# A graph layer with sorted edges: the first nodes' words loaded earlier and in two parts, a group of nodes multiplied tile by tile, the last group scaled from PSUM

## The chip, the cores and the metric

The kernel runs on one core of a Trainium2 chip. A core has five queues of instructions that work side by side: TensorE (PE, matrix products into PSUM), VectorE (DVE), ScalarE (ACT), GpSimd (POOL) and SyncE (SP, which here issues DMAs). The metric is the device time of one execution in microseconds, as the median of several.

## What is computed

The input is a graph of 12,500 nodes with 128 numbers each and 412,500 directed edges (200,000 random pairs in both directions, and a loop at every node). The edges are sorted by their target node `dst`. Cut to what matters, with all constant factors left out:

```
f0 = x[:, :32] @ W1_0e            f1 = x[:, 32:] (as 32 x 3) @ W1_1o
feat0, self0 = halves of f0       feat1, self1 = halves of f1
e0, e1 = feat0[src], feat1[src]                          # a gather, one row an edge
h = gelu(gelu(edge_attr_8 @ W_mlp1) @ W_mlp2)            # edge weights
w00, w01, w10, w11 = h @ Wp_00, h @ Wp_01, h @ Wp_10, h @ Wp_11
mid0 = [w00 * e0 * a0,   w11 * sum(e1 * a1)]             # a0, a1: edge_attr_4
mid1 = [w01 * e0 * a1,   w10 * e1 * a0]
n0, n1 = segment_sum(mid0, dst), segment_sum(mid1, dst)  # sums by target node
y = [cos * self0 + sin * (n0 @ W2_0e),  cos * self1 + sin * (n1 @ W2_1o)]
out = layernorm(x + y)
```

## The kernel before

**Pieces.** The sorted edges are cut into 806 runs of 512 (`SB`) edges; the last run has 340. Four runs (`CH`) make a chunk, so there are 202 chunks (`NCH`), and the nodes are cut into 25 groups of 512 (`GN`), each of four tiles of 128; the last group has 128 + 84 nodes. A loop over steps `s` (L946) takes one run a step; `c, k = divmod(s, CH)`.

**Setup** (L897 to L941) is a loop over `b` from 0 to 26. Step `b` turns the nodes of group `b` with TensorE, multiplies those of group `b - 1` by the feature weights, stores those of group `b - 2` to the `table` in DRAM through ScalarE's queue, and loads the nodes of group `b + 6` through SP. From `b = 5` on it also takes one load from the list that `weight_loads` makes (L908, L924), and at some steps one extra piece of work: `load_raws(0)` at 4, `load_indices(0)` at 12, `make_w1b` at 15, `tile_places` at 21 (L910 to L914). Meanwhile GpSimd gathers the rows of the first 18 runs straight from `x`. After setup it gathers from `table`, up to 18 runs ahead of the run in work; the order of the instructions on PE, ACT, DVE and SP is the order of the program (L896).

**A step of the main loop.** GpSimd gathers the rows of run `s + 18`, four gathers of 128 rows; in some runs a column of 128 rows comes instead from ScalarE or VectorE, which copy single columns out of the transposed nodes `xT` (L190, L192), or from single-row DMAs on SP (L209). TensorE makes the edge weights of later runs (L521 to L569). VectorE multiplies weights and gathered rows into messages `M` (L637, L641), and TensorE sums the messages of run `s - 1` by target node (L666, L668). Where in the sums the 128 edges of a column begin is read from `tile_first`, the first target node of each column; the relative node of an edge, `rel`, lies in 0 to 7 (`J` = 8) and picks one of eight places. Per chunk, VectorE adds the sums of 96 nodes to an accumulator of 768 nodes (L681) at `first_at`, the first node of the chunk less a base.

**Groups of nodes.** When the last edges of a group are in, `norm` multiplies its nodes: `moments` (L687) makes one TensorE product with `xT` (L698) and four with the accumulator (L701) for each tile, into one PSUM tile, and ScalarE copies that to SBUF (L706, L708). Later `statistics` takes mean and variance (L714, L715), `deviations` the root, and `normalise` scales the tiles on ScalarE (L742; for the last group, every second on VectorE, L739) and stores them through SP (L744). Group 23, the last but one, is multiplied at chunk 200, and group 24 after the last chunk, in `norm_last`.

**One buffer used several times in setup.** `scratch` (L319) is the first buffer of the accumulator, 128 rows of 4 x 768 words. Until the main loop's step 1 it holds what setup needs:

```
return scratch[:, part, :SB]                                        # L446 rows_tile(part)
raws[b] = [load_run_rows(dst, b, NO_NODE, None if b else 0), ...]   # L449 load_raws: dst in part 0, src in part 1
return scratch.rearrange("p a n -> p (a n)").bitcast(dtype)[0:1, i * NCH:(i + 1) * NCH]   # L323 line(i)
first_node = line(0, I32)                                           # L325
```

`load_raws(0)` brings the targets of runs 0 to 127, one run a row. `load_indices(0)` casts them to floats (L457), subtracts the first of each 128 (L460) and turns them into `rel`. `first_node` holds the first target of each of the 202 chunks and is read by `find_first` at step 1 (L402).

**The branch at the end.** The scheme needs edges sorted by target, with at most eight different nodes in 128 edges. `load_indices` counts the edges that break this: words below the first of their 128 (L461) and words at least 7.5 above it (L463), both into `odd`; `find_first` and `tile_places` count places out of range. `count_odd` sums the counts (L783), and at the end

```
with tc.If(n_odd > padded):    # L1041
    general()
```

where `padded` is 44, the words that fill up the last run. `general` (L788) does all edges again in any order: it zeroes sums in DRAM, runs a loop over 412,500 / 125 = 3,300 passes (L805), each of which loads 125 edges (L810 to L813), gathers their rows (L822) and the old sums (L880), makes weights and messages, and scatters the new sums (L884), and then normalises all groups again.

Of the kernel before, what the change touches and what calls it, by code (L numbers as in the profile page):

```python
# [25 lines left out]
Q = 4  # L26
# [25 lines left out]
COL_Q = {DVE: Q - 2, ACT: Q - 3}  # L52
COL_FROM = {DVE: 12, ACT: 12}
LNB = 2
TURN_AT = (7, 9, 11, 13, 15, 17, 18, 20, 22, 24)


@with_exitstack
def gnn_kernel(ctx: ExitStack, tc: tile.TileContext, x, src, dst, ea4, ea8, w1_0, w1_1, wm1, wm2,
# [26 lines left out]
    def sub(ap, offset, dims):  # L86
        return bass.AP(tensor=ap.tensor, offset=ap.offset + offset, ap=dims)
# [248 lines left out]

    def weight_loads():

        yield w1r, sub(wm1, 0, [[0, P // RAD], [HID, RAD], [1, HID]])
        yield w2b, sub(wm2, 0, [[0, 2], [HID, HID], [1, HID]])  # L340
        for j, w in enumerate((wp00, wp01, wp10, wp11)):
            yield wpb[:, j * MUL:(j + 1) * MUL], sub(w, 0, [[0, 2], [MUL, HID], [1, MUL]])
        for t, w in ((w20, w2_0), (w21, w2_1)):
            yield t[:MUL, :], w[:MUL, :]
            yield t[MUL:, :], sub(w, MUL * MUL, [[0, 3], [MUL, MUL], [1, MUL]])
        yield first_node, sub(dst, 0, [[1, 1], [CH * SB, NCH]])
        for b, t in enumerate(tile_first):
            c0, n = b * P, t.shape[0]
            last = c0 + n == NCH and E < NCH * CH * SB
            if last:  # L350
                yield (t[n - 1:n, :].rearrange("a (k o) -> a k o", o=1),
                       sub(dst, (NCH - 1) * CH * SB, [[1, 1], [0, CH * Q], [1, 1]]))
                k = -(-(E - (NCH - 1) * CH * SB) // P)
                yield t[n - 1:n, :k], sub(dst, (NCH - 1) * CH * SB, [[k * P, 1], [P, k]])
            yield t[:n - last], sub(dst, c0 * CH * SB, [[CH * SB, n - last], [P, CH * Q]])

    def make_w1b():

# [31 lines left out]
    assert all(len(bs) == 1 for c, bs in due.items() if c < NCH - 1)  # L390
    assert N - base[-1] + SPAN <= ACC and ACC - GN <= GN
    first_at = cst.tile([1, NCH], I32)
    NT = -(-NCH // P)
    tile_first = [cst.tile([min(P, NCH - b * P), CH * Q], I32, name=f"tf{b}") for b in range(NT)]

    def find_first():

        floor, strays = line(1), line(2)
        steps = [(0, 0)] + [(c + 1, (bs[-1] + 1) * GN) for c, bs in due.items() if c + 1 < NCH]
        for (r, n0), (z, _) in zip(steps, steps[1:] + [(NCH, 0)]):  # L400
            nc.vector.memset(floor[:, r:z], float(n0))
        nc.vector.tensor_tensor(floor, first_node, floor, op=OP.subtract)  # L402
        nc.vector.tensor_scalar(strays, floor, 0.0, float(ACC - SPAN), op0=OP.max, op1=OP.min)
        nc.vector.tensor_copy(first_at, strays)
        nc.vector.tensor_tensor(strays, strays, floor, op=OP.not_equal)
        nc.vector.tensor_reduce(odd[0:1, 2 * NB:2 * NB + 1], strays, axis=mybir.AxisListType.X, op=OP.add)

    def tile_places():

        for b, t in enumerate(tile_first):  # L410
# [233 lines left out]

    def places(c):

        b, r = divmod(c, P)
# [34 lines left out]


    pend, done = [], []
    before_last = due[NCH - 1][0] - 1

    def moments(b, sums=None):  # L687
        n0, nn, full, tail, tiles = group(b)
        if not pend:
            Y["y"] = wk.tile([P, LNB, XB, P], F32, name="y", bufs=1)  # L690
            Y["v"] = wk.tile([P, LNB * XB, 2], F32, name="mv")
            nc.vector.memset(Y["v"], 1.0)
        j = len(pend)
        pend.append(b)
        pt = ps.tile([P, XB, P], F32, name="h")
        at = n0 - base[-1] if b in due[NCH - 1] else 0
        for t, k in tiles:
            nc.tensor.matmul(pt[:k, t, :], xT[:, n0 + t * P:n0 + t * P + k], ws, start=True, stop=sums is not None)  # L698
            if sums is None:
                for a in range(4):  # L700
                    nc.tensor.matmul(pt[:k, t, :], A["now"][:, a, at + t * P:at + t * P + k], wpost[:, a, :],  # L701
                                     start=False, stop=a == 3)
            else:
                nc.vector.tensor_tensor(pt[:k, t, :], pt[:k, t, :], sums[:k, t, :], op=OP.add)
        if full:
            nc.scalar.activation(Y["y"][:, j, :full, :], pt[:, :full, :], AF.Copy)  # L706
        if tail:
            nc.scalar.activation(Y["y"][:tail, j, full, :], pt[:tail, full, :], AF.Copy)  # L708

    def statistics(b):  # L710
        j = pend.index(b)
        st = wk.tile([P, XB, 6], F32, name="bst")
        for t, k in group(b)[4]:
            nc.vector.bn_stats(st[:k, t, :], Y["y"][:k, j, t, :])  # L714
            nc.vector.bn_aggr(Y["v"][:k, j * XB + t, :], st[:k, t, :])  # L715

    def deviations():
# [5 lines left out]
    def normalise(last=False, keep=False):  # L723
        y, mv, a = Y["y"], Y["v"], Y["rs"]
        i0, n = len(done) * XB, len(pend) * XB
        v, r, u, m = (a[:, i, i0:n] for i in range(4))
        nc.vector.reciprocal(r, u)

        nc.vector.tensor_tensor(u, r, r, op=OP.mult)
        nc.vector.scalar_tensor_tensor(u, v, -0.5, u, op0=OP.mult, op1=OP.mult)  # L730
        nc.vector.scalar_tensor_tensor(r, u, 1.5, r, op0=OP.add, op1=OP.mult)
        nc.vector.scalar_tensor_tensor(m, mv[:, i0:n, 0], -1.0, r, op0=OP.mult, op1=OP.mult)
        for j, b in enumerate(pend):
            if b in done:
                continue
            for t, k in group(b)[4]:
                i = j * XB + t - i0
                if last and t % 2:
                    nc.vector.tensor_scalar(y[:k, j, t, :], y[:k, j, t, :], r[:k, i:i + 1], m[:k, i:i + 1],  # L739
                                            op0=OP.mult, op1=OP.add)  # L740
                    continue
                nc.scalar.activation(y[:k, j, t, :], y[:k, j, t, :], AF.Identity,  # L742
                                     bias=m[:k, i:i + 1], scale=r[:k, i:i + 1])
            store_nodes(nc.sync, out, b, y[:, j])  # L744
        done[:] = pend if keep else []
        if not keep:
            pend.clear()

    def norm(bs):
        for b in bs:  # L750
            moments(b)
            move_sums()
            new_sums()

# [11 lines left out]
    def norm_last(bs):  # L766
        for b in bs:
            moments(b)
            statistics(b)
            if len(pend) == LNB:  # L770
                deviations()
                normalise(True)
        if len(pend) > len(done):
            deviations()
            normalise(True)

    odd_f = cst.tile([1, 1], F32)
    odd_i = cst.tile([1, 1], I32)
# [117 lines left out]
    with tc.manual_schedule(engines={PE, ACT, DVE, SP}):  # L896
# [7 lines left out]
        for b in range(min(AHEAD, NG)):  # L904
# [41 lines left out]
        for s in range(NCH * CH + CH):  # L946
# [120 lines left out]
```

## Time and profile before

| | |
|---|---|
| time, median of 3 runs | 3552.09 us (3550.64 to 3557.92) |
| profiled execution | 3556.29 us |
| its span in the profile | 3554.4 us |
| granted TensorE clock, mean | 0.932 |
| busy: PE, DVE, ACT, POOL | 89%, 88%, 79%, 75% of the span |
| DMA | 239.29 MB, mean 67 GB/s |

A row of a group names line, engine, operation, output <- inputs, and how many, then the busy time in us, the mean of one in ns, and the idle time of the engine just before, with what ended it. A row in order of time has the start and the duration in us, and in brackets the idle time before it. A row of a single line gives least, median and greatest duration in ns, and first and last start in us. A queue's own instructions (SPq, ACTq, POOLq, PEldq) issue DMAs, wait or branch; the time of a DMA row there is that of its issue.

### The profile page before, as it was taken

Reading aid. Unit: us, or ns where it says so; the run is one execution under the profiler, and the core shown is the slowest. Engines: PE = TensorE matmul, PEld = TensorE weight load, DVE = VectorE, ACT = ScalarE, POOL = GpSimd, SP = SyncE. Lnnn points to the kernel's source line nnn. Section 1 sums busy time; section 2 is a strip of 40 time slices with the busy share of each in tenths; the row PEclk is TensorE's granted clock in tenths of the full one; section 3 lists DMA queues with packets and bytes.
Section 4 is the critical chain, followed back from the end, with each engine's and each line's share of the span. In section 5 each row is a group of like instructions: output and inputs, shape, how many; then the busy total and the mean of one; then the engine's idle time right before and its main releaser. Section 6 shows DMA issues by size and latency. Waiting matters only on the chain. (4 is left out here: it accounts for less than half of the span.)

```text
span 3554.4 us, 143693 instructions
## 1 busy us (share of the span) xinstructions
PE 3159.9 (89%) x28598; PEld 2755.6 (78%) x28598; DVE 3129.2 (88%) x29317; ACT 2797.6 (79%) x23671; POOL 2667.6 (75%) x2804
## 2 busy tenths in 40 slices
PE   6899898998898988998899898898899989888888
PEld 6777777787777777877788787787787777777777
DVE  2699999999999999999899899888899888889897
ACT  3488788788888888887887888877787887788785
POOL 7777777777777777777777777777777777777775
PEclk8999999998999999899998899989899999999998
DMA  8322332223322223322323323323323232232221
GB/s 199 70 62 68 63 64 65 63 61 74 64 60 67 63 60 74 64 60 62 68 61 70 67 59 64 65 63 68 65 62 64 59 69 63 60 69 63 60 65 47
DMA packets 579225, 239.29 MB, mean 67 GB/s; under 512 B 483651, under 2 KB 528747, under 8 KB 578347
## 3 DMA queue, kind: packets, MB, share of 16 engines
q0 software_dynamic: 89536, 183.55, 20.3%
q1 hardware_dynamic: 468041, 40.02, 9.1%
q10 hardware_dynamic: 20770, 6.47, 0.8%
q8 instruction: 252, 4.13, 0.5%
q14 instruction: 626, 5.13, 0.5%
HBM read 217.00 MB, written 12.80 MB: 65 GB/s over the span
## 5 line engine op out<-in xcount | busy, mean ns | idle before, releaser
L222 POOL DMA_INDIRECT G<-table,idx x2726 | 2598.9, 953 | 836.7 <-issue 718.5
L192 ACT ACTIVATE gt<-xT 128x1 f32 x22016 | 2166.7, 190 | 73.3 <-issue 53.6
L190 DVE COPY gt<-xT 128x1 f32 x25216 | 1728.6, 144 | 212.1 <-issue 172.9
L666 PE MATMUL sums<-own,M 128*128 128x96 f32 x6446 | 1354.8, 294 | 74.3 <-DVE M L641 73.0
L668 PE MATMUL sums<-own,M 128*128 128x96 f32 x6446 | 1319.7, 288 | 85.1 <-DVE M L641 84.1
L666 PEld LDWEIGHTS sums<-own,M 128*128 128x128 f32 x6446 | 1037.5, 201 | 181.9 <-DVE M L641 101.7
L668 PEld LDWEIGHTS sums<-own,M 128*128 128x128 f32 x6446 | 1035.3, 202 | 108.9 <-DVE M L641 107.6
L641 DVE TENSOR_TENSOR M<-w,G 128x384 f32<-128x384 f32 x1612 | 880.1, 547 | 0.0
L569 PE MATMUL w<-wpb,h 64*128 64x128 f32 x6448 | 649.3, 305 | 57.8 <-DVE M L641 56.3
L569 PEld LDWEIGHTS w<-wpb,h 64*128 64x128 f32 x6448 | 496.5, 197 | 199.6 <-issue 74.3
L637 DVE TENSOR_TENSOR M<-w,G 128x256 f32<-128x256 f32 x806 | 333.4, 414 | 34.4 <-issue 19.9
L540 ACT ACTIVATE h<-h 128x512 f32<-128x512 f32 x404 | 216.3, 586 | 178.6 <-PE h L536 165.7
L536 PE MATMUL h<-eT,w1b 64*128 64x128 f32 x3232 | 288.7, 319 | 8.4 <-ACT e L523 8.3
L536 PEld LDWEIGHTS h<-eT,w1b 64*128 64x128 f32 x3232 | 241.3, 218 | 38.7 <-ACT e L523 13.7
L556 ACT ACTIVATE h<-h 128x512 f32<-128x512 f32 x404 | 213.5, 577 | 26.3 <-PE h L551 22.5
L551 PE MATMUL h<-h,w2b 64*64 64x256 f32 x3232 | 222.6, 391 | 0.0
L199 ACT ACTIVATE G<-h 128x128 f32<-128x128 f32 x369 | 96.4, 277 | 120.5 <-PE h L198 76.4
L198 PE MATMUL h<-wf,gt 128*128 128x128 f32 x738 | 143.5, 294 | 1.9 <-ACT h L556 0.9
L529 ACT ACTIVATE eT<-h 128x128 f32<-128x128 f32 x202 | 56.0, 277 | 112.7 <-PE h L527 89.5
L551 PEld LDWEIGHTS h<-h,w2b 64*64 64x64 f32 x3232 | 104.5, 133 | 44.8 <-issue 0.5
L630 DVE TENSOR_TENSOR own<-oh,e 128x512 f32<-128x512 f32 x202 | 137.6, 681 | 0.7 <-issue 0.2
L681 DVE TENSOR_TENSOR acc<-sums,acc 128x384 f32 x202 | 111.2, 550 | 9.7 <-issue 6.2
(113 smaller groups left out, 1329.1 us busy)
## 6 DMA issues: line engine op xcount, KB each, us to landing
G<-table SPq DMA_DIRECT2D x7168, 0.5 KB
G<-table,idx POOLq DMA_INDIRECT x2726
e<-in_edge_attr SPq DMA_DIRECT2D x201, 64.0 KB
own<-in_x SPq DMA_DIRECT2D x24, 256.0 KB
table<-acc ACTq DMA_DIRECT2D x24, 256.0 KB
xt<-in_edge_attr SPq DMA_DIRECT2D x24, 256.0 KB
out<-y SPq DMA_DIRECT2D x24, 256.0 KB
xt<-in_dst SPq DMA_DIRECT2D x5, 256.0 KB
```

Source lines behind the costliest of these rows:

```text
L190: nc.vector.tensor_copy(to, col)
L192: nc.scalar.activation(to, col, AF.Copy)
L222: nc.gpsimd.indirect_dma_start(out=G[s][:, q, :], out_offset=None, in_=x if s < raw_runs else table, in_offset=bass.IndirectOffsetOnAxis(a ...
L536: nc.tensor.matmul(p1[h][:, j // 2, j % 2, :], w1b[rows, j, :], eT[c][rows, :], start=True, stop=True)
L540: nc.scalar.activation(H1[c][h], p1[h].rearrange("p k j e -> p (k j e)"), AF.Gelu_apprx_tanh, scale=1.0 / math.sqrt(RAD))
L551: nc.tensor.matmul(p2[r][k * HID:(k + 1) * HID, h * n:(h + 1) * n], w2b[rows, :], H1[c][h][rows, k * n:(k + 1) * n], start=True, stop=True)
L556: nc.scalar.activation(H2[c][r].rearrange("p k j e -> p (k j e)"), p2[r], AF.Gelu_apprx_tanh, scale=1.0 / math.sqrt(HID))
L569: nc.tensor.matmul(WP[i][:, q, :], H2[c][q % 2][rows, k, q // 2, :], wpb[rows, :], start=True, stop=True)
L637: nc.vector.tensor_tensor(M[s][:, :, :, :MUL], w[:, :, :2 * MUL].rearrange("p q (a u) -> p q a u", a=2), g[:, :, None, :MUL].to_broadcast( ...
L641: nc.vector.tensor_tensor(M[s][:, :, j, MUL:].rearrange("p q (i u) -> p q i u", i=3), w[:, :, None, (2 + j) * MUL:(3 + j) * MUL].to_broadc ...
L666: nc.tensor.matmul(flat[:, bass.ds(at, 4 * FIRST_HALF)].bitcast(F32), M[s][:, q, 0, :], own[:, 3 * WIDE:], start=False, stop=False)
L668: nc.tensor.matmul(sb[:, 1:, bass.ds(at, 4 * WIDE)].bitcast(F32), M[s][:, q, 1, :], own[:, :3 * WIDE].rearrange("p (a j) -> p a j", a=3), ...
```

## The change

1. `first_node` and the words of tiles of the first 16 chunks (`FIRST_TILES`) become the first entries of the list of weight loads; the words of the other chunks, now in tiles of 128 and 58 chunks, are loaded behind the loads of `late` at the start of the main loop and turned into places at step 9 instead of in setup. `places` picks the tile by its first chunk.
2. Group 23 is multiplied tile by tile: tiles 0 to 2 at the steps `k == 3` of chunks 194, 196 and 198, when the chunks that can reach them are in, and tile 3 where the whole group was; each has its own PSUM tile and its own copy. `find_first` bounds the places of the chunks behind them so that they can't reach an earlier tile.
3. For group 24 the copies out of PSUM go away: statistics and scaling read PSUM. Its full tile is stored through ScalarE's queue, its tail through SP's.

```diff
     def weight_loads():
 
+        yield first_node, sub(dst, 0, [[1, 1], [CH * SB, NCH]])
+        yield from tile_loads(0)
         yield w1r, sub(wm1, 0, [[0, P // RAD], [HID, RAD], [1, HID]])
...
-        yield first_node, sub(dst, 0, [[1, 1], [CH * SB, NCH]])
-        for b, t in enumerate(tile_first):
...
+    def tile_loads(b):
+
+        t, c0 = tile_first[b], tile_from[b]
+        n = t.shape[0]
+        last = c0 + n == NCH and E < NCH * CH * SB
...
+        yield t[:n - last], sub(dst, c0 * CH * SB, [[CH * SB, n - last], [P, CH * Q]])
...
-    NT = -(-NCH // P)
-    tile_first = [cst.tile([min(P, NCH - b * P), CH * Q], I32, name=f"tf{b}") for b in range(NT)]
+    tile_from = [0, *range(FIRST_TILES, NCH, P)]
+    NT = len(tile_from)
...
+    before_last = due[NCH - 1][0] - 1
+    done_at = [math.ceil((before_last * GN + (t + 1) * P + MARGIN) / N * NCH) - 1 for t in range(XB)]
...
+        for t, (a, z) in enumerate(zip(done_at, done_at[1:])):
+            nc.vector.tensor_scalar(strays[:, a + 1:z + 1], strays[:, a + 1:z + 1], float((t + 1) * P), None, op0=OP.max)
...
-    def moments(b, sums=None):
+    def moments(b, sums=None, part=None):
         n0, nn, full, tail, tiles = group(b)
+        if part is not None:
+            tiles = tiles[part:part + 1]
...
+        if sums is None and b == NG - 1:
+            Y["pt"] = pt
+            return
+        if part is not None:
+            nc.scalar.activation(Y["y"][:, j, part, :], pt[:, part, :], AF.Copy)
+            return
...
+    def rows_of(b, j, t, k):
+        return Y["pt"][:k, t, :] if b == NG - 1 and "pt" in Y else Y["y"][:k, j, t, :]
...
-            nc.vector.bn_stats(st[:k, t, :], Y["y"][:k, j, t, :])
+            nc.vector.bn_stats(st[:k, t, :], rows_of(b, j, t, k))
...
+                z = rows_of(b, j, t, k)
...
+                if last:
+                    eng = nc.sync if t % 2 else nc.scalar
+                    eng.dma_start(out[b * GN + t * P:b * GN + t * P + k, :], y[:k, j, t, :])
+            if not last:
+                store_nodes(nc.sync, out, b, y[:, j])
...
-            moments(b)
+            moments(b, part=XB - 1 if b == before_last else None)
...
-                 NG // 2 + 9: tile_places, NG // 2 + 10: lambda: mlp2(1), NG // 2 + 11: make_ws, NG: make_wpost}
+                 NG // 2 + 9: lambda: tile_places([0]), NG // 2 + 10: lambda: mlp2(1), NG // 2 + 11: make_ws, NG: make_wpost}
...
-        late = list(aid_load())
+        late = list(aid_load()) + [load for b in range(1, NT) for load in tile_loads(b)]
...
+            if k == 3 and c - 1 in done_at[:-1]:
+                moments(before_last, part=done_at.index(c - 1))
...
+            if s == 9:
+                tile_places(range(1, NT))
```

More of the change, by code (lines that the diff above doesn't have):

```diff
@@ L54 @@
 LNB = 2
+FIRST_TILES = 16
 TURN_AT = (7, 9, 11, 13, 15, 17, 18, 20, 22, 24)
@@ L345, in weight_loads @@
             yield t[MUL:, :], sub(w, MUL * MUL, [[0, 3], [MUL, MUL], [1, MUL]])
-        yield first_node, sub(dst, 0, [[1, 1], [CH * SB, NCH]])
-        for b, t in enumerate(tile_first):
[L348 to L355, printed above, removed]
+    def tile_loads(b):
[3 more added lines that the diff above has]
+        if last:
+            yield (t[n - 1:n, :].rearrange("a (k o) -> a k o", o=1),
+                   sub(dst, (NCH - 1) * CH * SB, [[1, 1], [0, CH * Q], [1, 1]]))
+            k = -(-(E - (NCH - 1) * CH * SB) // P)
+            yield t[n - 1:n, :k], sub(dst, (NCH - 1) * CH * SB, [[k * P, 1], [P, k]])
+        yield t[:n - last], sub(dst, c0 * CH * SB, [[CH * SB, n - last], [P, CH * Q]])
     def make_w1b():
@@ L392, in gnn_kernel @@
     first_at = cst.tile([1, NCH], I32)
-    NT = -(-NCH // P)
-    tile_first = [cst.tile([min(P, NCH - b * P), CH * Q], I32, name=f"tf{b}") for b in range(NT)]
+    tile_from = [0, *range(FIRST_TILES, NCH, P)]
+    NT = len(tile_from)
+    tile_first = [cst.tile([z - a, CH * Q], I32, name=f"tf{b}")
+                  for b, (a, z) in enumerate(zip(tile_from, tile_from[1:] + [NCH]))]
+    before_last = due[NCH - 1][0] - 1
+    assert len(due[NCH - 1]) == 1
+    done_at = [math.ceil((before_last * GN + (t + 1) * P + MARGIN) / N * NCH) - 1 for t in range(XB)]
+    assert due[done_at[-1]] == [before_last] and done_at == sorted(set(done_at))
+    assert not any(c in due for c in range(done_at[0] - 1, done_at[-1])) and done_at[-1] < NCH - 2
     def find_first():
@@ L406, in find_first, with tile_places @@
         nc.vector.tensor_reduce(odd[0:1, 2 * NB:2 * NB + 1], strays, axis=mybir.AxisListType.X, op=OP.add)
-    def tile_places():
-        for b, t in enumerate(tile_first):
+    def tile_places(bs):
+        for b in bs:
+            t = tile_first[b]
             n = t.shape[0]
@@ L645, in places @@
     def places(c):
-        b, r = divmod(c, P)
+        b = max(b for b, a in enumerate(tile_from) if a <= c)
+        r = c - tile_from[b]
         _, PLACE[c] = nc.values_load_multi_w_load_instructions(
@@ L684, in gnn_kernel @@
     pend, done = [], []
-    before_last = due[NCH - 1][0] - 1
-    def moments(b, sums=None):
+    def moments(b, sums=None, part=None):
         n0, nn, full, tail, tiles = group(b)
+        if part is not None:
+            tiles = tiles[part:part + 1]
         if not pend:
@@ L692, in moments @@
             nc.vector.memset(Y["v"], 1.0)
-        j = len(pend)
-        pend.append(b)
+        if b not in pend:
+            pend.append(b)
+        j = pend.index(b)
         pt = ps.tile([P, XB, P], F32, name="h")
@@ L737, in normalise @@
                 i = j * XB + t - i0
+                z = rows_of(b, j, t, k)
                 if last and t % 2:
-                    nc.vector.tensor_scalar(y[:k, j, t, :], y[:k, j, t, :], r[:k, i:i + 1], m[:k, i:i + 1],
+                    nc.vector.tensor_scalar(y[:k, j, t, :], z, r[:k, i:i + 1], m[:k, i:i + 1],
                                             op0=OP.mult, op1=OP.add)
[L741 to L744, printed above, removed]
+                else:
+                    nc.scalar.activation(y[:k, j, t, :], z, AF.Identity,
+                                         bias=m[:k, i:i + 1], scale=r[:k, i:i + 1])
+                if last:
+                    eng = nc.sync if t % 2 else nc.scalar
+                    eng.dma_start(out[b * GN + t * P:b * GN + t * P + k, :], y[:k, j, t, :])
+            if not last:
+                store_nodes(nc.sync, out, b, y[:, j])
         done[:] = pend if keep else []
@@ L775, in norm_last @@
             normalise(True)
+        Y.pop("pt")
     odd_f = cst.tile([1, 1], F32)
```

## The prediction, made before the changed kernel ran

> **What bounds the kernel now.** I read the page first, then the order in time on each queue around the places that the change touches.
>
> ```profile
> span 3554.4 us, 143693 instructions
> ...
> L222 POOL DMA_INDIRECT G<-table,idx x2726 | 2598.9, 953 | 836.7 <-issue 718.5
> ```
>
> ```profile
> 92.74 0.94 POOL L222 DMA_INDIRECT G<-in_x,idx_raw  x1 [0.30 <-issue]
> 99.37 0.94 POOL L222 DMA_INDIRECT G<-table,idx  x1 [5.68 <-DVE M L641]
> ...
> 3528.32 0.94 POOL L222 DMA_INDIRECT G<-table,idx  x1 [0.30 <-issue]
> ```
>
> The reader sees a GpSimd queue that never rests: from 99.37 to 3528.32 it issues 2,726 gathers, 1.26 us apart, each 0.95 us of work and about 0.30 us of issue. The one real hole is the 5.68 us ahead of the first gather from the table. So GpSimd bounds the main loop, and the end is its last gather (3529.26) plus a tail of 25.1 us. The profiled execution took 3556.29 us (span 3554.4), 4.2 us above the median of 3552.09; durations come from it, the forecast starts from the median.
>
> **The change part by part. First the order of the loads,** because what it does to memory outweighs every duration. Setup takes one load per step from `weight_loads`, beginning at step 5. The change puts `first_node` at the head of that list. `first_node` is `line(0)` (L325): row 0, words 0 to 201, of `scratch`. The same buffer holds the raw destinations of the first 128 runs: `load_raws(0)` (step 4) writes them to `scratch[:, 0, :512]`, so run 0 is row 0, words 0 to 511. They are read only at step 12, by the cast at L457. In the kernel before, the eleventh load came at step 15, when that row had been used:
>
> ```profile
> 22.31 0.66 SPq L480 DMA_DIRECT2D acc<-in_dst  x1
> ...
> 25.74 0.70 SPq L925 DMA_DIRECT2D w1r<-in_L_gnn_W_mlp  x1
> ...
> 53.38 0.65 SPq L925 DMA_DIRECT2D acc<-in_dst  x1
> ```
>
> ```profile
> L457 DVE CAST ft<-acc x2: 416/416/416, 41.6 to 44.7; 128x512 f32<-128x512 int32 x2
> ```
>
> The raw rows are loaded at 22.31 and cast at 41.6; `first_node` arrives after that, at 53.38. In the changed kernel it takes the slot of `w1r`, 25.74, between the load and the cast. It overwrites the destinations of the first 202 edges of run 0 with the first nodes of all 202 chunks, in program order, so no luck of timing avoids it.
>
> What follows is arithmetic on the reference's sorted list (412,500 edges over 12,500 nodes, 33 an edge list). The words now read 0, 63, 126, 191 and so on, about 62 apart, then the true ones, below 17. L461 counts words under the first of their 128, L463 words 8 or more above it. Of block 0, 127 words are counted; of block 1, which begins with word 128 of the list (near node 7,900), 73 that lie above and the 54 true ones that lie below. That is 254. The kernel's limit is `padded` = 44, and the 44 fill words of the last run use it up already. So n_odd is 298 against 44, and L1041 takes the branch to `general()`, which the run before passed over. That repeats all the edge work in 3,300 passes of 125 edges (T is the largest divisor of 412,500 up to 128).
>
> **A pass of the loop.** Nothing of it is in the trace; I bound it by the nearest rows. As compiled, a pass ends in a wait for every semaphore and two meetings of all engines, so passes don't overlap, and I add up the chain.
>
> ```profile
> 0.76 0.43 SPq L109 DMA_DIRECT2D idx_raw<-in_src  x1
> 3.84 1.09 POOL L222 DMA_INDIRECT G<-in_x,idx_raw  x1 [2.67 <-DMA idx_raw<-in_src]
> 5.64 0.66 PE L294 MATMUL w<-ident,own 128*128 128x128 f32 x2 [5.64 <-DMA own<-in_x]
> ...
> 52.97 0.59 ACT L295 ACTIVATE xT<-w 128x512 f32<-128x512 f32 x1
> 55.38 0.27 PE L527 MATMUL h<-ident,e 128*128 128x128 f32 x1
> 55.69 0.28 ACT L529 ACTIVATE eT<-h 128x128 f32<-128x128 f32 x1 [0.29 <-PE h L527]
> ...
> 95.65 0.18 DVE L379 TENSOR_SCALAR wpost<-w 32x32 f32<-32x32 f32 x1
> ...
> 117.90 5.17 SPq L209 DMA_DIRECT2D G<-table  x16
> ...
> 3545.09 1.04 PE L701 MATMUL h<-wpost,acc 128*84 128x128 f32 x8
> ```
>
> ```profile
> L925 SPq DMA_DIRECT2D wpb<-in_L_gnn_Wp x4: 539/612/834, 34.6 to 42.3; - x4
> ```
>
> ```profile
> 3452.30 2.32 DMA G<-table,idx
> ```
>
> ```profile
> L1041 SPq EVENT_SEMAPHORE  x8: 17/17/17, 3552.2 to 3552.8; - x8
> ...
> L1041 POOLq INC_SWDGE_SEM  x1: 1027/1027/1027, 3524.9 to 3524.9; - x1
> L1041 PEldq COMPARE_BRANCH  x1: 3879/3879/3879, 3544.6 to 3544.6; - x1
> ...
> L1041 SPq COMPARE_BRANCH  x1: 54/54/54, 3551.4 to 3551.4; - x1
> ```
>
> - Four loads on SP; the chain hangs on the fourth (`a8`). Three issues ahead of it at 0.61 (L925, 128 short rows): 1.84. From its issue to use 3.08, as from 0.76 to 3.84. At best 0.32 an issue (5.17 for 16, L209) and 2.32 (a gather's landing); at worst 4.39, the first load of x (from 1.25, six issues in one row, to 5.64). Taken: 4.9.
> - TensorE: six single steps (L825, L829, L833, L837, the last of L855, L871) at 0.27, the four of L860 at 1.04: 2.7.
> - ScalarE: four of 128 columns at 0.28, one of 512 at 0.59: 1.7.
> - VectorE: twelve small ones (L827, ten at L843 to L851, L883) at 0.18: 2.2.
> - Thirteen hand-overs between engines at 0.05 (L527 ends at 55.65, L529 begins at 55.69): 0.65.
> - The scatter at L884: 0.94 of GpSimd, 0.30 of issue, 2.32 to land: 3.6.
> - The meetings: SP needs 2.2 us from its first wait (3552.2) to the span's end (3554.4) for much the same; 1.03 more for GpSimd's increment of its semaphores, which all wait for: 3.2 (at best that 1.03 alone).
> - Two taken branches: 0.8 each, as SP spends from its branch at 3551.4 to its next instruction: 1.6 (at best 0.1 each; at worst the 3.88 of TensorE's row each).
>
> Both gathers, the index arithmetic and the activation table lie beside these. Sum: 20.5 us a pass, 67.8 ms for 3,300; with the lower ends 15.3 us (50 ms), with the upper ones 28 us (92 ms). Zeroing the sums ahead and 25 groups of norms behind I put at 0.2 ms.
>
> On the branches the Trainium skill ("Runtime: NRT & Kernel Launch", section "Instruction fetch mechanics") says that a taken branch stalls only when its target lies outside the two pages of code that an engine holds. This loop is short, so by that rule the 1.6 us would nearly vanish and a pass would take 19; the 3.88 us row was a jump over the whole of `general()`, which agrees.
>
> **The rest of the change, on the fast path.** These terms hold whether or not the loop runs.
>
> ```profile
> 66.80 8.94 SPq L496 DMA_DIRECT2D e<-in_edge_attr  x1
> ...
> 88.32 0.46 SPq L496 DMA_DIRECT2D e<-in_edge_attr  x1
> ```
>
> ```profile
> 81.75 1.08 ACT L540 ACTIVATE h<-h 128x512 f32<-128x512 f32 x2 [10.13 <-DMA pick<-in_src]
> ...
> 97.05 0.62 ACTq L262 DMA_DIRECT2D table<-acc  x1
> ```
>
> Late words of tiles: the same edge load issues in 0.46 us at 88.32 and in 8.94 at 66.80, right behind the words of 73 chunks. SP's later loads wait behind it, and ScalarE's store of the table waited 10.13 us for one of those. Moved behind the loop's start, that stall holds nobody: the table's last store goes out some 8.5 us sooner (8.94 less 0.46), near 89 instead of 97.05, and GpSimd, free at 93.7, no longer waits. Of its hole of 5.68, 0.30 stays: −5.4. The four loads more that SP issues at step 1, behind the sixteen of L959, have eight steps to land before step 9 reads them; twelve small VectorE instructions there (2.2 us) are covered by the 18 runs of gathers already ahead. If the store were still late, nothing is gained: −5.4 to 0.
>
> ```profile
> 3527.97 0.41 PE L698 MATMUL h<-ws,xT 128*128 128x128 f32 x2
> 3528.22 1.06 PE L701 MATMUL h<-wpost,acc 128*128 128x128 f32 x8
> 3529.11 0.39 PE L698 MATMUL h<-ws,xT 128*128 128x128 f32 x2
> ...
> 3536.21 0.42 DVE L637 TENSOR_TENSOR M<-w,G 128x256 f32<-128x256 f32 x1 [5.08 <-PE w L569]
> ```
>
> Group 23 by tiles: a tile costs TensorE 1.14 us (3527.97 to 3529.11). Three leave the stretch in which VectorE waits 5.08 us for TensorE: −3.4. They go to steps where GpSimd's pace covers them, with three ScalarE copies of 0.28 and a slot of PSUM each; should the last one, 26 us ahead of the wait, still count, −2.3.
>
> ```profile
> 3546.57 0.29 DVE L714 BATCH_NORM_STATS2 bst<-y 128x6 f32<-128x128 f32 x1 [1.94 <-ACT y L706]
> ...
> 3549.97 0.72 SPq L262 DMA_DIRECT2D out<-y  x1
> ```
>
> The last group: TensorE ends at 3546.13, so the statistics can start 0.4 us sooner without the copies; the second store no longer queues behind the first on SP: 0.5. Together −0.9, between −1.3 and 0. The Trainium skill ("PSUM — Partial Sum Buffer", section "PSUM bank collisions raise a hardware error") forbids two engines in one bank at once. Both tiles share a bank, so by it the two scalings go one after the other and −0.5 is left; no row here shows it.
>
> Fast path in all: −9.7, from 3552.1 to 3542.4. With the loop: 3.54 + 67.8 + 0.2 ms, 71,500 us.
>
> **The rivals.**
> 1. The fallback runs (forecast): 71,500 us, 54,000 to 96,000 by its bounds. For: addresses and order above. Within it a stall of 3.88 at both branches would give 26.7 us a pass, 92,000 us; against it, SP's own branch shows 0.8.
> 2. It doesn't run: the overwritten words are not read, or not counted. Then the three edits do what they say and the kernel is faster, 3,542 us. It decides at the 45th counted word. Against: 254 new ones.
> 3. As 2, but the table is no sooner complete, because a store now waits for the late words of tiles: −4.3, 3,548 us, within 0.2%.
>
> **How the numbers follow.** Rival 1 has 0.91 (0.11 of it outside 54,000 to 94,000), rival 2 0.07, rival 3 0.02. The range 54,000 to 94,000 so leaves out 0.2; it is the span of rival 1's bounds, cut a little at the top, where two stalls in every pass would have to meet. Repeated runs of this kernel lie within some 0.2% of each other, so that is the bound of "same": faster 0.07, same 0.02, slower 0.91.
>
> **What would show it.** Rows at L805 to L885, with gathers at L822 and L880 counted 3,300 times, on a span some twenty times as long; if they are there, the passes' period against 20.5 us tells which term was mis-sized. L925's load of `acc` near 26, ahead of L457's cast. On the fast path GpSimd's first gather from the table near 94 with 0.30 ahead of it, L698 four times in single tiles, and no L706 for the last group. A span near 3,545 with no row at L822 would prove the reading of memory wrong.

## The result, and the profile after

The changed kernel takes 65,872.8 us (median of 6 runs, 65,840.0 to 65,890.6) against 3,554.1 of the kernel before on the same chip: 18.53 times as long, interval 18.50 to 18.55. Of the experiments, f1, f2, f3, f4 and h4 ran on two other chips, on which the kernel before itself takes 5,534 and 5,544 us at a granted clock of 0.73, so each is read against that, or by its passes.

The page of the profile after, its span, busy times and granted clock:

```profile
span 65838.3 us, 676126 instructions
...
PE 25020.5 (38%) x101394; PEld 17391.8 (26%) x101394; DVE 17135.6 (26%) x92413; ACT 12646.7 (19%) x43611; POOL 14637.3 (22%) x12705
...
PEclk9955555555555555555555555555555555555555
```

No engine is busy for even 40% of the span. The first two of the 40 slices look like the kernel before; in the other 38 the clock is half. The groups of instructions say what runs there (lines of `general` lie 34 further down than in the kernel before):

```profile
L894 PE MATMUL h<-wpost,G 128*125 128x128 f32 x26400 | 6825.1, 438 | 1546.2 <-ACT G L891 1546.2
...
L914 POOL DMA_INDIRECT G<-sums,g_di x3300 | 3995.6, 1211 | 1006.3 <-DVE G L876 926.1 <-issue 79.9 <-DVE G L861 0.3
L918 POOL DMA_INDIRECT sums<-G,g_to x3300 | 3995.5, 1211 | 28453.2 <-DVE G L917 28453.2
...
L223 POOL DMA_INDIRECT G<-table,idx x2726 | 2596.9, 953 | 831.4 <-issue 651.1 <-DMA G<-table,idx 97.6 <-DVE M L657 36.6
```

The gather of old sums and the scatter (L914, L918) occur 3,300 times: the loop of `general()` ran from end to end, behind the 2,726 gathers of the normal way. Why is seen in setup, in order of time on SP and VectorE, with one row of the line that issues the listed loads:

```profile
22.04 0.65 SPq L496 DMA_DIRECT2D acc<-in_dst  x1
...
28.56 0.82 SPq L959 DMA_DIRECT2D acc<-in_dst  x1
...
44.15 0.42 DVE L473 CAST ft<-acc 128x512 f32<-128x512 int32 x1
```

```profile
L959 SPq EVENT_SEMAPHORE  x1: 17/17/17, 28.5 to 28.5; - x1
```

`first_node` (L959, into `acc`, the buffer of `scratch`) now goes out between the load of the raw destinations (L496) and their cast. SP even waits at 28.5, with the one semaphore wait of that line, until those destinations have landed: the two writes to one place are kept in order, and the wrong one comes last. Where the load goes to another place (h1 below), the line has no such wait, and the load goes out at 24.94.

### The profile page after: what moved, and what is told of

It is laid out like the page before. It is cut to its first block, busy times and chain, and to the rows that moved or that the text cites. A ratio compares the mean times of both kernels' runs of the same rounds, so it can differ in the third digit from the quotient of the medians.

```text
span 65838.3 us, 676126 instructions
## 1 busy us (share of the span) xinstructions
PE 25020.5 (38%) x101394; PEld 17391.8 (26%) x101394; DVE 17135.6 (26%) x92413; ACT 12646.7 (19%) x43611; POOL 14637.3 (22%) x12705
## 5 line engine op out<-in xcount | busy, mean ns | idle before, releaser
L918 POOL DMA_INDIRECT sums<-G,g_to x3300 | 3995.5, 1211 | 28453.2 <-DVE G L917 28453.2
L856 POOL DMA_INDIRECT G<-table,g_si x3300 | 3979.9, 1206 | 20722.0 <-DMA g_a<-in_edge_attr 18826.7
L894 PE MATMUL h<-wpost,G 128*125 128x128 f32 x26400 | 6825.1, 438 | 1546.2 <-ACT G L891 1546.2
L894 PEld LDWEIGHTS h<-wpost,G 128*125 128x125 f32 x26400 | 5844.7, 325 | 2497.7 <-ACT G L891 2497.7
L889 PE MATMUL w<-ident,G 125*128 125x125 f32 x13200 | 3520.4, 422 | 6212.7 <-DVE G L881 6212.7
L914 POOL DMA_INDIRECT G<-sums,g_di x3300 | 3995.6, 1211 | 1006.3 <-DVE G L876 926.1
L889 PEld LDWEIGHTS w<-ident,G 125*128 125x128 f32 x13200 | 2335.3, 216 | 7089.6 <-issue 7089.6
L877 DVE SCALAR_TENSOR_TENSOR G<-G,g_a 125x32 f32<-125x32 f32 x3300 | 830.9, 252 | 9157.4 <-ACT G L873 9157.4
L905 PE MATMUL h<-G 125*125 125x128 f32 x6600 | 2602.2, 497 | 1207.8 <-ACT G L896 1207.8
L871 PE MATMUL w<-wpb,G 64*125 64x128 f32 x6600 | 2587.6, 493 | 1181.4 <-ACT G L869 1181.4
L223 POOL DMA_INDIRECT G<-table,idx x2726 | 2596.9, 953 | 831.4 <-issue 651.1
L867 PE MATMUL h<-G,w2b 64*64 64x125 f32 x6600 | 2229.3, 438 | 1183.9 <-ACT G L865 1183.9
L885 DVE SCALAR_TENSOR_TENSOR G<-G,g_a 125x32 f32<-125x32 f32 x9900 | 2445.6, 247 | 0.0
L883 DVE SCALAR_TENSOR_TENSOR G<-G,g_a 125x32 f32<-125x32 f32 x9900 | 2445.0, 247 | 0.0
```

The lines of the kernel that those rows point to most:

```text
L223: nc.gpsimd.indirect_dma_start(out=G[s][:, q, :], out_offset=None, in_=x if s < raw_runs else table, in_offset=bass.IndirectOffsetOnAxis(a ...
L856: nc.gpsimd.indirect_dma_start(out=g, out_offset=None, in_=table, in_offset=bass.IndirectOffsetOnAxis(ap=si, axis=0))
L867: nc.tensor.matmul(p2, w2b[:HID, :HID], h1, start=True, stop=True)
L871: nc.tensor.matmul(pw, h2, wpb[:HID, :], start=True, stop=True)
L883: nc.vector.scalar_tensor_tensor(m[:, 1 + k, :MUL], w[:, MUL:2 * MUL], a4[:, 1 + k:2 + k], g[:, :MUL], op0=OP.mult, op1=OP.mult)
L885: nc.vector.scalar_tensor_tensor(m[:, 1 + k, r], w[:, 3 * MUL:], a4[:, 1 + k:2 + k], g[:, r], op0=OP.mult, op1=OP.mult)
```

## The experiments

**Which words, and whose.** The first two leave the overlap out in two ways.

```diff
 f1_line_moved
-    first_node = line(0, I32)
+    first_node = scratch.rearrange("p a n -> p (a n)").bitcast(I32)[0:1, 512:512 + NCH]
```

> The changed kernel with one line edited: `first_node` lies in words 512 to 713 of the scratch row and no longer in words 0 to 201, where the destinations of run 0 are. Loads, order and everything else stay. Theory (overwritten destinations are counted and the branch is taken): 44 counted words against a limit of 44, no loop, and the three edits alone are left: 3,544 us (-9.7 against the kernel before: loads -5.4, tiles -3.4, last group -0.9), and no gather in the loop. Rival A (the count comes from another part: the bounds of the places, or the tiles now taken in at step 9): 65,870 us as before the edit. Rival B (the early issue itself upsets a later load): 65,870 us too.

```diff
 f3_late_in_list
-        yield first_node, sub(dst, 0, [[1, 1], [CH * SB, NCH]])    # ahead of tile_loads(0)
...
+        yield first_node, sub(dst, 0, [[1, 1], [CH * SB, NCH]])    # behind the ten weight loads
```

> The changed kernel with one entry of the list of loads moved: `first_node` is loaded behind the ten weight loads again, so that it reaches words 0 to 201 of the scratch row after the cast of the raw destinations; the words of the first 16 chunks stay at the head of the list. Theory: the row is whole when it is cast, no loop, 3,544 us. It is the second way out of the same overlap: place in f1_line_moved, time here. If only f1_line_moved were short and this one 65,870 us, the load's place in the list would not matter and the overlap would sit elsewhere. Rival A: 65,870 us.

The page of f1_line_moved begins:

```profile
span 5530.8 us, 143698 instructions
```

143,698 instructions and not 676,126: no pass ran. The times are 5,531.5 us (f1) and 5,527.7 (f3) beside 5,534.1 of the kernel before, ratios 0.9994 (0.9982 to 1.0006) and 0.9988 (0.9976 to 1.0). So the bounds of the places and the tiles taken in at step 9, which both kernels keep, don't bring the count over its limit (rival A), and f1, which loads just as early, clears the early issue (rival B). What the three edits gain did not show on that chip; h1 below has it.

```diff
 f4_before_head (the kernel before)
     def weight_loads():
 
+        yield first_node, sub(dst, 0, [[1, 1], [CH * SB, NCH]])
...
-        yield first_node, sub(dst, 0, [[1, 1], [CH * SB, NCH]])
```

> The kernel before with that one load alone put at the head of the list of weight loads; none of the change's other edits. Theory: the load overwrites the destinations of 202 edges, 254 more words are counted, and the loop runs: 65,840 us of the changed kernel and 8 us more for the missing edits, some 65,850. Rival A: the rest of the change makes the count, so 3,554 us.

```diff
 f2_one_word (the changed kernel)
-    first_node = line(0, I32)
+    first_node = scratch.rearrange("p a n -> p (a n)").bitcast(I32)[0:1, 511:511 + NCH]
```

> The changed kernel with `first_node` in words 511 to 712 of the scratch row, one word earlier than in f1_line_moved: exactly one destination of run 0, its last, is overwritten (by 0, far below the first of its 128). Theory: 45 counted words against a limit of 44, so the loop runs in full: 65,870 us, no less than for 254 words. Rival (the limit has slack, or the cost goes with the number of words hit): 3,544 us, or something in between.

The scatter's row in f4, by its line, and in f2, by the groups:

```profile
L884 POOL DMA_INDIRECT sums<-G,g_to x3300: 1210/1210/1222, 5558.9 to 67761.3; - x195
```

```profile
L918 POOL DMA_INDIRECT sums<-G,g_to x3300 | 3994.9, 1211 | 28609.5 <-DVE G L917 28609.5
```

Both run all 3,300 passes: 67,927.8 us and 67,964.1 (one run each). Less 5,534 that is 62,394 and 62,430, against 62,319 for the changed kernel (65,873 less 3,554). One moved entry of a list, in the kernel before, costs it all; and one overwritten word costs as much as 202. The limit has no slack, as the 44 fill words would have it.

**The three edits alone,** each on the kernel before; of the change's diff, the lines of one part.

```diff
 g1_loads_only: part 1, with first_node at word 512
+        yield first_node, sub(dst, 0, [[1, 1], [CH * SB, NCH]])
+        yield from tile_loads(0)
...
+        late = list(aid_load()) + [load for b in range(1, NT) for load in tile_loads(b)]
```

> The kernel before with the first part of the change alone (words of tiles in two parts, `first_node` early), `first_node` kept clear of the destinations at word 512. Theory: the 8.94 us load behind the words of 73 chunks no longer stands ahead of ScalarE's store of the table; GpSimd's hole ahead of the first gather from the table shrinks from 5.68 to 0.30 us: -5.4, 3,548 us. Rival (a store of the table now waits for the sixteen chunks' words or for another late load): 0, 3,553 us, the hole still over 5 us.

GpSimd in g1_loads_only, in order of time:

```profile
92.98 0.94 POOL L223 DMA_INDIRECT G<-in_x,idx_raw  x1 [0.31 <-issue]
94.22 0.94 POOL L223 DMA_INDIRECT G<-table,idx  x1 [0.30 <-DVE M L649]
```

The first gather from the table starts at 94.22 with 0.30 ahead of it, as foreseen. The time is 3,547.0 against 3,556.1, ratio 0.9974 (0.9964 to 0.9984), so −9.1 (−5.7 to −12.8) rather than −5.4. The idle time ahead of these gathers fell by 5.3 (836.7 to 831.4); the rest is the gathers' own sum, 2,594.7 for 2,598.9 us, which also differs between kernels that don't touch it (2,595.8 in g2, 2,597.2 in g3). Why it differs no run shows.

```diff
 g2_tiles_only: part 2
-            moments(b)
+            moments(b, part=XB - 1 if b == before_last else None)
...
+            if k == 3 and c - 1 in done_at[:-1]:
+                moments(before_last, part=done_at.index(c - 1))
```

> The kernel before with the second part alone (group 23 multiplied tile by tile). Theory: three tiles of 1.14 us leave the stretch in which VectorE waited 5.08 us for TensorE: -3.4, 3,550 us; -2.3 if the last of the three still counts. Rival (TensorE is not what ends that wait, since the edge weights' other work or a clock at half speed takes the room): 0, 3,553 us.

```profile
3530.83 0.42 DVE L645 TENSOR_TENSOR M<-w,G 128x256 f32<-128x256 f32 x1 [1.74 <-PE w L577]
```

VectorE's wait behind the last gathers is 1.74 and was 5.08: −3.3. The time is 3,551.1, ratio 0.9992 (0.9983 to 1.0001): the row shows the gain, the time alone doesn't.

```diff
 g3_psum_only: part 3
+        if sums is None and b == NG - 1:
+            Y["pt"] = pt
+            return
...
+                    eng = nc.sync if t % 2 else nc.scalar
```

> The kernel before with the third part alone (statistics and scaling of the last group from PSUM, its two stores on two queues). Theory: -0.9, 3,552.5 us: 0.4 for the copies ahead of the statistics, 0.5 for the second store. If the two scalings, from one bank of PSUM, go one after the other: -0.5. Rival (the tail from 3529 on is no shorter, since the store that goes through ScalarE's queue now waits for ScalarE): 0. All of these lie near what a measurement can tell; the rows of the last group decide.

The scalings of the last group's two tiles, first in the kernel before, then in g3_psum_only:

```profile
3548.93 0.34 DVE L739 TENSOR_SCALAR y<-y,rs 84x128 f32<-84x128 f32 x1
3548.99 0.49 ACT L742 ACTIVATE y<-y,rs 128x128 f32<-128x128 f32 x1 [1.09 <-DVE rs L732]
```

```profile
3547.69 0.46 ACT L749 ACTIVATE y<-h,rs 128x128 f32<-128x128 f32 x1 [1.03 <-DVE rs L738]
...
3548.18 0.41 DVE L746 TENSOR_SCALAR y<-h,rs 84x128 f32<-84x128 f32 x1 [0.53 <-ACT y L749]
```

From SBUF the two engines ran side by side; from PSUM VectorE waits 0.53 us for ScalarE. The Trainium skill ("PSUM — Partial Sum Buffer", section "PSUM bank collisions raise a hardware error") forbids two engines in one bank at once; the row agrees. The time is 3,555.1, ratio 0.9999 (0.999 to 1.0008): within the spread.

The same kernel as f1_line_moved, no further edit:

> The same kernel as f1_line_moved, to be timed where the kernel before takes its usual 3,550 to 3,560 us. The three parts alone gave -9.1, -5.1 and -1.0 in their medians (with intervals of some 3.5 us each way), and in their traces -5.4 (GpSimd's hole), -3.5 (the stretch behind the last gather) and -0.6. Theory (the parts add up once the loop is gone): -9.5 by the traces, 3,544 us, with GpSimd's first gather from the table at 94 and some 22.3 us from its last gather to the end. Rival (the parts lose to each other: GpSimd, earlier by 5.4, meets a VectorE that is no earlier): -5, 3,549 us, with a longer stretch behind the last gather.

```profile
86.24 0.85 ACTq L263 DMA_DIRECT2D table<-acc  x1
...
94.08 0.94 POOL L223 DMA_INDIRECT G<-table,idx  x1 [0.30 <-DVE M L657]
...
3515.41 0.17 DVE L818 TENSOR_REDUCE odd_f<-h 1x1 f32<-1x18 f32 x1 [2.19 <-PE h L817]
...
3520.04 0.94 POOL L223 DMA_INDIRECT G<-table,idx  x1 [0.30 <-issue]
...
3525.70 1.02 DVE L657 TENSOR_TENSOR M<-w,G 128x384 f32<-128x384 f32 x2
...
3529.28 0.42 DVE L653 TENSOR_TENSOR M<-w,G 128x256 f32<-128x256 f32 x1 [1.97 <-PE w L585]
```

VectorE's last messages ahead of the wait in the kernel before, and then a stretch of h1 by engines:

```profile
3529.52 1.01 DVE L641 TENSOR_TENSOR M<-w,G 128x384 f32<-128x384 f32 x2
```

```profile
3500.00:3510.00 10.00, 8.68 (x51) 7.82 (x51) 7.93 (x80) 5.50 (x47) 7.56 (x9) 0.66 0.22 55
```

All three edits without the loop: 3,546.0 against 3,553.1, −7.1, ratio 0.998 (0.9971 to 0.9989), the fastest version that was tried with all three. The table's last store goes out at 86.24 (97.05 in the kernel before), and the hole is closed. GpSimd's last gather begins 8.3 us earlier (3,520.04 for 3,528.32), but VectorE's last messages ahead of the wait begin 5.7 us behind it, and not 1.2 (3,529.52 in the kernel before). So 4.5 of the gain went, as the rival has it, into a VectorE that is no earlier: shortly before, TensorE stood at a granted clock of 0.66 (column before the last two of the windows row) and VectorE waited 2.19 for the count's product. The profile of the changed kernel has the same stretch, also at 0.66; with g1 alone it is at 0.83, with g2 alone at 1.00. The kernel before has such a stretch too, earlier (0.60 from 3,480 to 3,500), and VectorE has caught up by the end. Whether the clock makes the delay, and whether the edits cause it together, stays open.

**What a pass costs.** The pass in the changed kernel, in order of time, from one scatter to the next:

```profile
30008.76 1.21 POOL L918 DMA_INDIRECT sums<-G,g_to  x1 [8.57 <-DVE G L917]
...
30013.52 0.26 SPq L844 DMA_DIRECT2D g_si<-in_src  x1
...
30014.85 0.26 SPq L847 DMA_DIRECT2D g_a<-in_edge_attr  x1
...
30016.28 1.21 POOL L856 DMA_INDIRECT G<-table,g_si  x1 [6.32 <-DMA g_a<-in_edge_attr]
...
30016.52 0.37 PE L859 MATMUL h<-ident,g_a 125*8 125x125 f32 x1 [8.40 <-DMA g_a<-in_edge_attr]
...
30018.36 0.68 PE L867 MATMUL h<-G,w2b 64*64 64x125 f32 x2 [0.36 <-ACT G L865]
...
30020.52 0.25 DVE L877 SCALAR_TENSOR_TENSOR G<-G,g_a 125x32 f32<-125x32 f32 x1 [2.78 <-ACT G L873]
...
30023.81 2.07 PE L894 MATMUL h<-wpost,G 128*125 128x128 f32 x8 [0.47 <-ACT G L891]
...
30027.66 1.21 POOL L918 DMA_INDIRECT sums<-G,g_to  x1 [8.66 <-DVE G L917]
30032.39 1.28 ACT L865 ACT_TABLE_LOAD   x1 [6.20 <-PEq L839]
```

The loop's own line in the stretch 30,008 to 30,016, and its branches over the whole span:

```profile
L839 SPq EVENT_SEMAPHORE  x17: 17/28/9891, 30002.1 to 30015.5; - x17
...
L839 SPq DRAIN  x3: 7/7/7, 30012.5 to 30013.0; - x3
```

```profile
L839 PEldq COMPARE_BRANCH  x3302: 80/216/240, 3537.1 to 65678.0; - x195
...
L839 SPq COMPARE_BRANCH  x3302: 49/55/70, 3566.0 to 65677.4; - x195
```

SP's first wait, from 30,002.1, is the long one, 9.89 us: it ends at 30,011.9, when the scatter has landed. SP then goes through its other waits, drains its queue first at 30,012.5, and the next loads go out at 30,013.52, 1.6 us behind the landing (also in the mean of all passes).

```diff
 g4_T100 (the changed kernel)
-        T = max(t for t in range(1, P + 1) if E % t == 0)
+        T = max(t for t in range(1, 101) if E % t == 0)
```

> The changed kernel with passes of 100 edges in place of 125: 4,125 passes in place of 3,300, with the same edges in all. Theory (a pass costs what its chain of loads, hand-overs, scatter and meeting takes, whatever the number of its edges): (65,838 - 3,543 - 200) x 1.25 + 3,743 = 81,400 us. Rival (the cost goes with the edges: bytes, columns of the products, rows gathered): near 65,870 us.

The loop's first load, in the changed kernel and in g4_T100:

```profile
L844 SPq DMA_DIRECT2D g_si<-in_src x3300: 262/263/294, 3566.5 to 65659.8; - x195
```

```profile
L844 SPq DMA_DIRECT2D g_si<-in_src x4125: 287/288/322, 3562.9 to 76230.1; - x197
```

The time is 76,408.8 us, between the theory (81,400) and the rival. A pass takes 17.62 us with 100 edges (the starts' distance by 4,124) and 18.82 with 125 (by 3,299): 0.048 us goes with each edge, so about 12.8 of 18.82 us go with the pass, by a line through these two points. Of the 1.20, 0.74 lie between the scatter and the next load (4.71 to 3.97, mean of all passes), 0.49 between first product and scatter. "Whatever the number of its edges" was too much.

```diff
 h3_fourth_first (the changed kernel; loads of a pass)
-si, di, a4, a8
+a8, di, si, a4
```

> The changed kernel with the four loads of a pass in another order: the eight edge features, on which the chain hangs, first and no longer fourth. Theory (issue to use takes 1.67 us and each issue ahead of it 0.445): the first product starts 1.33 us earlier, and the pass is 1.33 us shorter, 65,840 - 4,400 = 61,450 us. Rival (another load or the gather from the table, now later by up to 0.9, is next in line at the first message): -0.5 us a pass or less, 64,200 us or more.

```profile
30011.57 0.37 PE L859 MATMUL h<-ident,g_a 125*8 125x125 f32 x1 [7.11 <-DMA g_a<-in_edge_attr]
...
30013.54 1.21 POOL L856 DMA_INDIRECT G<-table,g_si  x1 [7.23 <-DVE G L876]
...
30017.06 0.25 DVE L877 SCALAR_TENSOR_TENSOR G<-G,g_a 125x32 f32<-125x32 f32 x1 [3.94 <-DMA G<-table,g_si]
```

The theory fell: 66,543.0 us, slower by 670. The first product does start 1.31 us earlier behind the pass's first load (1.66 for 2.97, mean), but the first message (L877) now waits for the gather, whose index load went from first to third. The rival named it; it cost more than the edit gained, 19.03 us a pass. From the gather's start to the message it took 3.52 us here (30,013.54 to 30,017.06) and 4.24 in the changed kernel, where it was not waited for: it had only some 0.7 us of cover there.

```diff
 h2_kept_busy, h4_no_rest (the changed kernel; 7 and 10, then 25 and 40 products)
             a8 = wk.tile([T, RAD], F32, name="g_a8")
...
+            fill = ps.tile([P, P], F32, name="h")
+            for _ in range(7):
+                nc.tensor.transpose(fill, ident, ident)
...
             nc.tensor.matmul(py, eq, y, start=True, stop=True)
+            fill = ps.tile([P, P], F32, name="h")
+            for _ in range(10):
+                nc.tensor.transpose(fill, ident, ident)
```

> The changed kernel, with 17 products of no use added to every pass of the loop, all in time in which TensorE waits: 7 at the pass's start, while the loads are under way (3.0 us), and 10 behind the pass's last product, while the scatter lands (4.4 us). Nothing waits for their results. Theory (the clock is granted at half because TensorE rests 8.6 us in each pass; the products then keep it at full): the steps on TensorE, 6.2 us of a pass at a granted clock of 0.50, fall to about half, -3.1 us a pass, 65,840 - 10,200 = 55,600 us, with a granted clock near 1. The Trainium skill (TensorE's page, on the clock gate) has the clock halved after an idle time of about 3.4 us; by it the longest rest that is left, under 3 us, keeps the clock full, the same 55,600. Rival (the half clock has another reason, or the share of busy time decides, which stays near one half): 65,840 us or up to 1.0 us a pass longer, 69,000, where the products reach over the waits.

```profile
20000.00:60000.00 40000.00, 22077.15 (x83196) 16389.11 (x83195) 9018.84 (x40531) 6335.93 (x12800) 7736.84 (x6399) 0.55 0.05 11
```

65,605.3 us: the clock (the third number from the end) is 0.55 in the loop, not 1. The test was weaker than meant: the added products took 0.21 us each, not 0.42, and left a rest of 3.6 us. Where the full clock came, it came for a single stretch of 3.41 us, which began between 0.3 us ahead of a scatter's start and 1.5 us behind it: the ten earned it, and it went by while the scatter landed.

> As h2_kept_busy, with 25 products of no use at a pass's start and 40 behind its last, since in h2_kept_busy the 7 and the 10 took 0.21 us each and left a rest of 3.6 us, and the full clock came for single stretches of 3.4 us, mostly while TensorE had nothing to do. Theory (continuous work earns the full clock, a rest loses it): at the full clock the added products take some 0.107 us each, 2.7 and 4.3 us, and fit into the two waits; the pass takes 18.82 - 3.1 = 15.7 us, 55,500 us in all. Rival A (the middle of a pass, where TensorE works 40% of the time, is enough of a rest to lose the clock again): full clock in a part of each pass, between 16 and 20 us a pass, 57,000 to 70,000 us. Rival B (the clock stays half whatever TensorE does here): the added products reach over both waits by 4.1 and 2.4 us, 25.3 us a pass, 87,300 us.

Windows of h4_no_rest, cut at the 3.41 us on which its clock changes; after the times stand TensorE's busy time, the granted clock, DMA share and GB/s:

```profile
40001.70:40005.11 3.41, 2.98 (x27) 1.00 0.02 6
40005.11:40008.53 3.42, 2.73 (x25) 1.00 0.08 2
40008.53:40011.94 3.41, 1.81 (x9) 1.00 0.08 19
40011.94:40015.35 3.41, 1.30 (x5) 0.50 0.07 19
40015.35:40018.77 3.42, 2.98 (x12) 0.50 0.00 0
40018.77:40022.18 3.41, 3.41 (x18) 0.50 0.08 19
```

A step of the same pass at the full clock, the one at L867 in the changed kernel:

```profile
40010.36 0.42 PE L870 MATMUL h<-G,w2b 64*64 64x125 f32 x2 [0.36 <-ACT G L868]
```

69,458.4 us, a clock of 0.80 in the loop, 19.32 us a pass: rival A. (A slower chip; but f2's pass on such a chip, 18.87 us, is nearly that of the changed kernel.) The half clock does come from TensorE's rests, and the pass's own middle, busy 1.81 of 3.41 us, is rest enough to lose the full clock again. In this pass 2.98 us of work at half clock didn't earn it back, 3.41 did. Over h4's whole loop the two borders are sharp: every window at full clock with less than 2.14 us of work lost it and every one with more than 2.30 kept it; at half clock none with less than 2.94 earned it and every one with more than 3.05 did. First product to scatter fell from 11.14 us to 10.21. Ahead of the first message hardly more was to be had, since it now waited for the gather from the table in 2,381 of the passes. The 40 products, part of them at half clock, reached past the scatter's landing and took 1.4 back.

## Why the prediction was right, and where its sizes were off

**The mechanism holds.** The load stands between the raw destinations and their cast; it goes out at 28.56 rather than near 26, since it waits for them. The count itself no run shows: 298 is arithmetic on the input, and f1 and f2 show the limit between no word and one. The branch is taken, the loop runs 3,300 times, and it takes 3,300 × 18.82 = 62.1 ms of the 62.3 added. Zeroing (3,543.0, SP's branch, to the first load at 3,566.5) and the norms (the last pass's end to 65,838) make the remaining 0.2, as put.

**The pass came out at 18.82 us against 20.5,** because errors of both signs met, which is luck:

| part of a pass | predicted | measured |
|---|---|---|
| first load to first product | 4.9 | 3.0 |
| TensorE's steps | 2.7 | 6.2 |
| ScalarE's, VectorE's steps | 3.9 | 4.0 |
| hand-overs | 0.65 | 0.9 |
| scatter until landed | 3.6 | 3.2 |
| meetings and branches | 4.8 | 1.6 |

The measured column is read from the pass above, with the rows left out there: 6.2 is 0.37, 0.65, 0.68, 0.78, 0.89 (from the last message to the end of the turns that follow), 2.07 and 0.79; 3.2 is 30,008.76 to 30,011.9, and 1.6 from there to 30,013.52.

The terms that failed are three. *Meetings and branches* were taken from the program's end, where SP needs 2.2 us, GpSimd's increment 1.03 and a branch 0.8; in the loop a branch takes 0.05 to 0.22 and the whole turn, with the waits that SP goes through, 1.6. The rule that the prediction cites from the Trainium skill ("Runtime: NRT & Kernel Launch", section "Instruction fetch mechanics") pointed the right way: by it the branches' 1.6 nearly vanish, and the trace agrees. *The loads* were priced by three issues at 0.61 and a load at the program's start; in the loop an issue comes every 0.445 and the fourth's data is used 1.67 after it. *TensorE's steps* were priced at the full clock, at one instruction each. L894 takes 2.07 us where the same eight instructions took 1.04, and a step like L867 is two instructions, 0.68 and not 0.27. At the full clock, in the first half of h4's pass, such a step took 0.42. With 1.03 us of L894 and 0.1 to 0.4 of each other step, read so from h4, some 2.7 of the 3.5 us are the clock (an estimate). The trace of before had half-clock stretches (a mean of 0.932); the prediction did not ask what a loop full of waits does to the clock. The Trainium skill ("TensorE: Matmul & The Clock Gate", section "Part 1: The HAM clock gate (the "warmup" mystery)") gives half clock as the state to which TensorE falls back when idle, decided in windows of about 3.4 us. The 0.50 of the loop and h4's windows agree; that a window more than half busy (1.81 of 3.41 us) loses the clock is what these runs add.

**That both gathers lie beside the chain** held for the one from the table by 0.7 us only, as h3 shows.

**The fast path** was put at −9.7; with the overlap gone it is −7.1 (−3.9 to −10.3), an interval that holds −9.7 too. By the rows, part 1 closed the hole to 0.30, part 2 took 3.3 off the wait, and part 3 brought a few tenths (from TensorE's last product to the end of the span 8.0 us for 8.3, from GpSimd's last gather 25.6 for 26.1), about the lower of its two prices. What the prediction left out is VectorE's delay near the end.

## What to carry to other kernels

When a load is moved, list everything that lives in its destination between the new place and the old, above all in a buffer that several parts of setup share: ordered writes prove no more than that the last one wins. A guard whose limit the padding already fills goes off at the first wrong word, and the price of what it guards then decides the time, so look at that price before moving anything it reads. For a loop of short waits like this one, take TensorE at half its clock and the turn of the loop from a loop's own rows, not from the program's end.

## What the runs showed of the hardware that was not expected

The clock is granted in stretches of 3.41 us and multiples, at 1 or 0.5 and nothing between: h2's ten products earned it 1,758 times in 3,300 passes, each time for one stretch, when TensorE had little left to do (0.98 us of it at most). A turn of this loop, with all engines meeting, costs 1.6 us behind the landing of the scatter, and a taken branch inside it 0.05 to 0.22 us.
